# A graph-attention layer: a one-hot pass in front, and the full attention in a dynamic loop behind a test that every block fails

## The chip, the cores and the metric

One core of one Trainium2 chip. The metric is the device time of one execution in microseconds (us), median of several. The profiles come from one execution each; a span is 2 to 4 us shorter than the time of its own run. Engines: TensorE (PE, with its weight loads as PEld), VectorE (DVE), ScalarE (ACT), GpSimd (POOL), SyncE (SP, which here computes nothing and issues most of the DMAs).

## The reference, cut to what matters

```python
def reference(x, adj, W, a):                 # x 4096x512, adj 4096x4096, W 512x(4*512), all float32
    ht  = (x @ W).reshape(N, 4, 512).transpose(1, 0, 2)
    src = einsum('hnd,hd->hn', ht, a[:, :512, 0]);  dst = einsum('hnd,hd->hn', ht, a[:, 512:, 0])
    e   = leaky_relu(src[:, :, None] + dst[:, None, :], 0.01) + adj[None]
    return layernorm(x + mean_over_heads(softmax(e) @ ht))
```

About one entry of adj in 256 is not zero, and those run up to 1e9, while the scores are of the order of tens. So in most rows the largest entry of adj decides the softmax alone. A row's *lead* is how far its largest entry of adj stands above the second.

## The kernel before

It applies the attention rows to x, which stays on chip, and then W. A unit of work is a block of 128 rows with one head. Its scores are made, 512 columns at a time, while the unit before it is in the matrix products:

```python
def add(self, c):        # scores of chunk c, and their largest in each row
    nc.scalar.activation(s, dst_b[:, h, ts(c, C)], AF.Identity, bias=src[:, ib, h : h + 1])
    nc.vector.scalar_tensor_tensor(s, s, SLOPE, s, op0=OP.mult, op1=OP.max)
    nc.vector.tensor_tensor_reduce(out=s, in0=s, in1=adj_t[ib, k][:, ts(part, C)], ...)
    if h == H - 1 and part == AW - 1 and ib + 1 < NB:
        load_adj(ib + 1, k)                  # adj of the next block, as soon as this tile is read
...
for n in range(len(units) + 1):              # 128 units in ONE stream
    after = Unit(n + 1) if n + 1 < len(units) else None
    for c in range(NCH):
        u.transpose(c)                       # 4 transposes, copied by VectorE or ScalarE
        ...                                  # c == 0: before.apply(7), before.scale(); 1: turn; 2: project; 3: store
        u.apply(c - 1)                       # 4 products with x
        after.add(c + 1)                     # scores of the next unit
        ...                                  # its maxima and exponentials at c == 6 and 7
    before, u = u, after
```

Of the kernel before, what the change touches and what calls it, by code (L numbers as in the profile page):

```python
# [9 lines left out]
F32 = mybir.dt.float32  # L10
AF = mybir.ActivationFunctionType
OP = mybir.AluOpType
# [4 lines left out]
LOWEST = -3.4028234663852886e38  # L17


@with_exitstack  # L20
def gat_resnorm_kernel(
# [8 lines left out]
    """layernorm(x + mean_h softmax(leaky_relu(src_i + dst_j) + adj) @ (x @ W_h)).  # L30

    The attention rows are applied to x first and the result to W_h after it:
    x stays on chip for the whole launch, x @ W would not fit. Likewise
    src = x @ (W_h a_src) and dst = x @ (W_h a_dst).
    A unit of work is a block of 128 rows of one head. Its scores are made in
    chunks of 512 columns while the unit before it is in the matrix products.
    """
    nc = tc.nc
    P = 128
    N, D = x.shape  # L40
    H = a.shape[0]
    KB = D // P          # blocks of features
    NB = N // P          # blocks of rows
    C = 512              # columns of a chunk
    NCH = N // C
    Q = C // P           # blocks of rows in a chunk
    AW = 2               # chunks in a tile of adj

    ctx.enter_context(tc.manual_schedule())

    const = ctx.enter_context(tc.tile_pool(name="const", bufs=1))
    x_sb = const.tile([P, NB, D], F32, name="x_sb")
    w_sb = const.tile([P, KB, H * D], F32, name="w_sb")
    dst_b = const.tile([P, H, N], F32, name="dst_b")
    src = const.tile([P, NB, H], F32, name="src")
    ident = const.tile([P, P], F32, name="ident")

    x_blocks = x.rearrange("(nb p) d -> p nb d", p=P)
    w_blocks = W.rearrange("(kb p) m -> p kb m", p=P)

# [1 line left out]
    with ExitStack() as pre:  # L62
        once = pre.enter_context(tc.tile_pool(name="once", bufs=1))
        two = pre.enter_context(tc.tile_pool(name="two", bufs=2))
        pps = pre.enter_context(tc.tile_pool(name="pps", bufs=2, space=bass.MemoryType.PSUM))

        a_b = once.tile([P, H, 2 * D], F32, name="a_b")
        nc.scalar.dma_start(
            a_b.rearrange("p h m -> p (h m)"),
            bass.AP(tensor=a.tensor, offset=a.offset, ap=[[0, P], [1, H * 2 * D]]),  # L70
        )
        for kb in range(KB):
            nc.scalar.dma_start(w_sb[:, kb, :], w_blocks[:, kb, :])
        for g in range(NCH):
            nc.sync.dma_start(x_sb[:, ts(g, Q), :], x_blocks[:, ts(g, Q), :])
        make_identity(nc, ident)

        v = once.tile([P, KB, 2 * H], F32, name="v")
        prod = once.tile([P, D], F32, name="prod")
        for kb in range(KB):  # L80
            for s in range(2):
                for h in range(H):
                    nc.vector.scalar_tensor_tensor(  # L83
                        prod, w_sb[:, kb, ts(h, D)], 1.0, a_b[:, h, ts(s, D)],
                        op0=OP.mult, op1=OP.mult,
                        accum_out=v[:, kb, s * H + h : s * H + h + 1],
                    )

        def x_transposed(g):
            xT = two.tile([P, KB, C], F32, name="xT")  # L90
            for q in range(Q):
                ps = pps.tile([P, KB, P], F32, name="ps_x")
                for kb in range(KB):
                    nc.tensor.transpose(ps[:, kb, :], x_sb[:, g * Q + q, ts(kb, P)], ident)  # L94
                nc.scalar.copy(xT[:, :, ts(q, P)], ps)  # L95
            return xT

        def scores(g, xT):
# [15 lines left out]
        xT = x_transposed(0)  # L114
        for g in range(NCH):
            ahead = x_transposed(g + 1) if g + 1 < NCH else None
            scores(g, xT)
            xT = ahead

# [1 line left out]
    adj_pool = ctx.enter_context(tc.tile_pool(name="adj_pool", bufs=1))  # L121
# [5 lines left out]
    psum = ctx.enter_context(tc.tile_pool(name="psum", bufs=2, space=bass.MemoryType.PSUM))  # L127

    units = [(ib, h) for ib in range(NB) for h in range(H)]
    adj_t, o_ps, norm = {}, {}, {}  # L130

    def load_adj(ib, k):
        t = adj_pool.tile([P, AW * C], F32, name=f"adj{k}")
        nc.sync.dma_start(t, adj[ts(ib, P), ts(k, AW * C)])
        adj_t[ib, k] = t

    class Unit:
        def __init__(self, n):
            self.ib, self.h = units[n]
            self.s = []  # L140
            self.m = stat.tile([P, NCH], F32, name="m")
            self.z = stat.tile([P, NCH], F32, name="z")
            self.nm = stat.tile([P, 1], F32, name="nm")
            self.rz = stat.tile([P, 1], F32, name="rz")
            self.pt = {}
            self.y_ps = None

        def add(self, c):
            """leaky_relu(src + dst) + adj, and its largest in each row."""
            ib, h = self.ib, self.h  # L150
            s = s_pool.tile([P, C], F32, name="s")
            self.s.append(s)
            nc.scalar.activation(s, dst_b[:, h, ts(c, C)], AF.Identity, bias=src[:, ib, h : h + 1])  # L153
            nc.vector.scalar_tensor_tensor(s, s, SLOPE, s, op0=OP.mult, op1=OP.max)  # L154
            k, part = divmod(c, AW)
            nc.vector.tensor_tensor_reduce(  # L156
                out=s, in0=s, in1=adj_t[ib, k][:, ts(part, C)], scale=1.0, scalar=LOWEST,
                op0=OP.add, op1=OP.max, accum_out=self.m[:, c : c + 1],
            )
            if h == H - 1 and part == AW - 1 and ib + 1 < NB:  # L160
                load_adj(ib + 1, k)

        def largest(self):
            nc.vector.tensor_reduce(self.nm, self.m, axis=AX.X, op=OP.max, negate=True)  # L164

        def exp(self, c):
            s = self.s[c]
            nc.scalar.activation(s, s, AF.Exp, bias=self.nm, accum_out=self.z[:, c : c + 1])  # L168

        def transpose(self, c):  # L170
            ps = psum.tile([P, Q, P], F32, name="pt_ps", bufs=3)
            for q in range(Q):
                nc.tensor.transpose(ps[:, q, :], self.s[c][:, ts(q, P)], ident)  # L173
            pt = pt_pool.tile([P, Q, P], F32, name="pt")
            if c in (1, 3, 5):
                nc.scalar.copy(pt, ps)  # L176
            else:
                nc.vector.tensor_copy(pt, ps)  # L178
            self.pt[c] = pt

        def apply(self, c):
            if c == 0:
                self.y_ps = psum.tile([P, D], F32, name="y_ps")
            pt = self.pt.pop(c)
            for q in range(Q):
                nc.tensor.matmul(  # L186
                    self.y_ps, pt[:, q, :], x_sb[:, c * Q + q, :],
                    start=(c == 0 and q == 0), stop=(c == NCH - 1 and q == Q - 1),
                )

        def scale(self):
            """The softmax's divisor, with that of the mean over heads."""
            nc.vector.tensor_reduce(self.rz, self.z, axis=AX.X, op=OP.add)
            nc.vector.tensor_scalar_mul(self.rz, self.rz, float(H))
            nc.vector.reciprocal(self.rz, self.rz)
            self.y = y_pool.tile([P, D], F32, name="y")
            nc.vector.tensor_scalar_mul(self.y, self.y_ps, self.rz)  # L197

        def turn(self):
            ps = psum.tile([P, KB, P], F32, name="yt_ps", bufs=1)  # L200
            for kb in range(KB):
                nc.tensor.transpose(ps[:, kb, :], self.y[:, ts(kb, P)], ident)  # L202
            self.yt = yt_pool.tile([P, KB, P], F32, name="yt")
            nc.scalar.copy(self.yt, ps)  # L204

        def project(self):
            ib, h = self.ib, self.h
            if h == 0:
                o_ps[ib] = psum.tile([P, D], F32, name="o_ps")
            for kb in range(KB):  # L210
                nc.tensor.matmul(  # L211
                    o_ps[ib], self.yt[:, kb, :], w_sb[:, kb, ts(h, D)],
                    start=(h == 0 and kb == 0), stop=(h == H - 1 and kb == KB - 1),
                )
            if h == H - 1:
                r = y_pool.tile([P, D], F32, name="y")
                nc.vector.tensor_add(r, o_ps.pop(ib), x_sb[:, ib, :])  # L217
                st = stat.tile([P, nc.vector.BN_STATS_DIM], F32, name="st")
                nc.vector.bn_stats(st, r)
                mv = stat.tile([P, nc.vector.BN_AGGR_DIM], F32, name="mv")  # L220
                nc.vector.bn_aggr(mv, st)
# [11 lines left out]

    for k in range(NCH // AW):
        load_adj(0, k)
    u = Unit(0)
    for c in range(NCH):
        u.add(c)
    u.largest()
# [61 lines left out]
```

## Time and profile before

| | before |
|---|---|
| median of 2 runs | 4705.72 us |
| busy: TensorE, VectorE, ScalarE | 98%, 45%, 39% |
| time per unit, per block of 4 units | 35.47 us, 141.9 us |
| start to the first load of adj of the attention part | 132.6 us |
| mean granted clock of TensorE | 0.992 |

In the rows of a group, the last two fields are the busy time with the mean length of one, and the idle time of the engine just before the group with what ended it. A row of a timeline gives start, length, engine, source line, operation and operands, and in brackets how long the engine had sat idle and what released it. The lines that carry the reading stand in the prediction below.

### The profile page before, as it was taken

The numbers are of one execution on the slowest core, as the hardware profiler recorded it, in microseconds if no ns is written. First come the engines' busy times: TensorE is split into PE (matmuls) and PEld (weight loads), VectorE is DVE, ScalarE is ACT, GpSimd is POOL, SyncE is SP. The second block draws the span as 40 slices with busy tenths as digits, with TensorE's granted clock in tenths as the row PEclk, the third lists the DMA queues.
The fourth block names the chain that finished last, engine by engine and source line by source line (L and its number), as shares of the span: only waits on it lengthen the run. The fifth ranks groups of instructions, "written<-read, shape, count | busy, mean of one in ns | idle before, by whom it ended". The sixth has DMA issues, their size and how long they took to land.

```text
span 4702.5 us, 38848 instructions
## 1 busy us (share of the span) xinstructions
PE 4596.1 (98%) x14112; PEld 2251.0 (48%) x14112; DVE 2124.3 (45%) x4656; ACT 1811.9 (39%) x3712; POOL 18.2 (0%) x38
## 2 busy tenths in 40 slices
PE   7899999999999999999999999999999999999999
PEld 3344444444444444444444444444444444444444
DVE  3444444444444444444444444444444444444443
ACT  1334334334334434433433433433433443343342
POOL 0000000000000000000000000000000000000000
PEclk7999999999999999999999999999999999999999
DMA  3000000000000000000000000000000000000000
GB/s 125 27 12 21 18 21 20 12 12 21 18 21 20 7 16 21 18 21 16 7 21 21 18 21 16 7 21 21 18 21 12 12 21 21 18 21 12 12 21 3
DMA packets 26127, 92.66 MB, mean 20 GB/s; under 512 B 2768, under 2 KB 2768, under 8 KB 25296
## 3 DMA queue, kind: packets, MB, share of 16 engines
q1 hardware_dynamic: 22656, 75.51, 4.7%
q0 software_dynamic: 2560, 8.39, 0.5%
q10 hardware_dynamic: 720, 6.29, 0.3%
q8 instruction: 111, 1.82, 0.2%
q14 instruction: 80, 0.66, 0.0%
HBM read 81.79 MB, written 8.39 MB: 19 GB/s over the span
## 4 chain that ended last, share of the span: by engine, by line
issue 75%; PE 23%; DVE 1%; POOL 0%; DMA 0%; ACT 0%; POOLq 0%; ACTq 0%; DVEq 0%
PE y_ps L186 16%; PE o_ps L211 2%; PE pt_ps L173 2%; PE ps_b L107 1%; PE ps_sd L101 1%; PE ps_x L94 0%; DVE y L197 0%; DVE prod L83 0%; PE yt_ps L202 0%; POOL out_dram L232 0%; DMA w_sb<-in_L_gnn_W_dram 0%; DVE s L154 0%; DVE sd L103 0%; DVE s L156 0%; PE ps_s L111 0%
## 5 line engine op out<-in xcount | busy, mean ns | idle before, releaser
L186 PE MATMUL y_ps<-x_sb,pt 128*128 128x512 f32 x8192 | 3685.7, 593 | 0.0
L186 PEld LDWEIGHTS y_ps<-x_sb,pt 128*128 128x128 f32 x8192 | 1487.1, 190 | 1531.3 <-issue 1530.9
L154 DVE SCALAR_TENSOR_TENSOR s<-s 128x512 f32<-128x512 f32 x1024 | 705.6, 689 | 1048.4 <-ACT s L153 1006.2
L153 ACT ACTIVATE s<-dst_b,src 128x512 f32<-128x512 f32 x1024 | 723.0, 718 | 971.2 <-PE pt_ps L173 952.2
L178 DVE COPY pt<-pt_ps 128x512 f32<-128x512 f32 x640 | 442.6, 692 | 997.4 <-PE pt_ps L173 997.4
L168 ACT ACTIVATE s<-s,nm 128x512 f32<-128x512 f32 x1024 | 724.0, 708 | 181.0 <-DVE nm L164 181.0
L173 PEld LDWEIGHTS pt_ps<-ident,s 128*128 128x128 f32 x4096 | 512.5, 141 | 551.7 <-issue 538.7
L176 ACT COPY pt<-pt_ps 128x512 f32<-128x512 f32 x384 | 225.1, 586 | 1346.4 <-PE pt_ps L173 1346.4
L156 DVE CUSTOM_DVE_ANT_0 s<-s,adj 128x512 f32<-128x512 f32 x1024 | 708.6, 692 | 35.1
L173 PE MATMUL pt_ps<-ident,s 128*128 128x128 f32 x4096 | 615.3, 273 | 12.7 <-ACT s L168 12.7
L211 PE MATMUL o_ps<-w_sb,yt 128*128 128x512 f32 x1024 | 460.8, 593 | 0.7 <-ACT yt L204 0.7
L211 PEld LDWEIGHTS o_ps<-w_sb,yt 128*128 128x128 f32 x1024 | 184.6, 190 | 184.6 <-issue 183.6
L197 DVE TENSOR_SCALAR y<-y_ps,rz 128x512 f32<-128x512 f32 x128 | 96.0, 750 | 296.8 <-PE y_ps L186 296.8
L168 ACT ACTIVATION_READ_ACCUMULATOR s<-s,nm 128x1 f32 x1024 | 191.2, 187 | 0.0
L202 PE MATMUL yt_ps<-ident,y 128*128 128x128 f32 x512 | 83.9, 286 | 52.6 <-DVE y L197 52.6
L204 ACT COPY yt<-yt_ps 128x512 f32<-128x512 f32 x128 | 75.0, 586 | 76.0 <-PE yt_ps L202 76.0
L202 PEld LDWEIGHTS yt_ps<-ident,y 128*128 128x128 f32 x512 | 53.6, 140 | 83.5 <-DVE y L197 83.5
L224 ACT ACTIVATE sd<-sd 128x1 f32<-128x1 f32 x32 | 6.5, 203 | 210.8 <-DVE sd L223 210.8
L156 DVE DVE_READ_ACCUMULATOR2_ANT m<- 128x1 f32 x1024 | 83.8, 82 | 0.0
L217 DVE TENSOR_TENSOR y<-o_ps,x_sb 128x512 f32<-128x512 f32 x32 | 22.1, 692 | 90.2 <-PE o_ps L211 90.2
L94 PE MATMUL ps_x<-ident,x_sb 128*128 128x128 f32 x128 | 29.9, 422 | 21.8 <-DMA x_sb<-in_x_dram 16.6
L95 ACT COPY xT<-ps_x 128x512 f32<-128x512 f32 x32 | 18.7, 586 | 76.8 <-PE ps_x L94 76.8
(31 smaller groups left out, 412.8 us busy)
## 6 DMA issues: line engine op xcount, KB each, us to landing
adj<-in_adj_dram SPq DMA_DIRECT2D x128, 512.0 KB, 3.4
x_sb<-in_x_dram SPq DMA_DIRECT2D x8, 1024.0 KB, 17.9
out_dram<-y POOLq DMA_DIRECT2D x32, 256.0 KB, 2.3
w_sb<-in_L_gnn_W_dram ACTq DMA_DIRECT2D x4, 1024.0 KB, 10.7
a_b<-in_L_gnn_a_dram ACTq DMA_DIRECT2D x1, 2048.0 KB, 8.8
```

Source lines behind the costliest of these rows:

```text
L153: nc.scalar.activation(s, dst_b[:, h, ts(c, C)], AF.Identity, bias=src[:, ib, h : h + 1])
L154: nc.vector.scalar_tensor_tensor(s, s, SLOPE, s, op0=OP.mult, op1=OP.max)
L156: nc.vector.tensor_tensor_reduce(out=s, in0=s, in1=adj_t[ib, k][:, ts(part, C)], scale=1.0, scalar=LOWEST, op0=OP.add, op1=OP.max, accum_o ...
L168: nc.scalar.activation(s, s, AF.Exp, bias=self.nm, accum_out=self.z[:, c : c + 1])
L173: nc.tensor.transpose(ps[:, q, :], self.s[c][:, ts(q, P)], ident)
L176: nc.scalar.copy(pt, ps)
L178: nc.vector.tensor_copy(pt, ps)
L186: nc.tensor.matmul(self.y_ps, pt[:, q, :], x_sb[:, c * Q + q, :], start=(c == 0 and q == 0), stop=(c == NCH - 1 and q == Q - 1),)
L197: nc.vector.tensor_scalar_mul(self.y, self.y_ps, self.rz)
L202: nc.tensor.transpose(ps[:, kb, :], self.y[:, ts(kb, P)], ident)
L204: nc.scalar.copy(self.yt, ps)
L211: nc.tensor.matmul(o_ps[ib], self.yt[:, kb, :], w_sb[:, kb, ts(h, D)], start=(h == 0 and kb == 0), stop=(h == H - 1 and kb == KB - 1),)
```

## The change

The new kernel first runs a one-hot pass. For each row it finds the largest entry of adj, gathers that row of x, projects and norms it. It then tests for each row whether the lead is larger than anything the scores could add. Blocks in which a row fails would be computed again by the full attention, inside a dynamic loop. In this version the lead asked for is overwritten with 1e30, so every row of every block fails.

```diff
+    leading_rows(tc, x, adj, W, a, out, ident, w_sb, v, n_bad, any_bad)
+    flag = nc.values_load(any_bad[0:1, 0:1], min_val=0, max_val=N)
+    with tc.If(flag > 0, preferred_fallthrough_block=False):
+        general(tc, x, adj, out, ident, w_sb, v, n_bad)
 ...                                         # leading_rows(), new:
+        nc.vector.tensor_scalar(lead_by, lead_by, 0.0, 1e30, op0=OP.mult, op1=OP.add)
 ...
+    for t in range(NB + LAG + 1):           # LAG = 2
+        if t < NB:
+            find_segment(t); row_norm(t)    # reduce 4096 columns to 64 segments, gather the best segment
+        if 0 <= t - 1 < NB:
+            find_column(t - 1)              # the column in it; gather that row of x
+        if 0 <= t - LAG < NB:
+            project(t - LAG); norm(t - LAG)
+        if t < KB:
+            head_vector(t)
 ...                                         # general(): x reloaded, preamble without its look-ahead
-        for g in range(NCH):
-            ahead = x_transposed(g + 1) if g + 1 < NCH else None
-            scores(g, xT)
 ...                                         # block(ib): the old pipeline, but over the 4 units of one block
-    for n in range(len(units) + 1):
+        for n in range(H + 1):
 ...
+    with tc.For_i(0, NB, 1) as ib:
+        here = nc.values_load(n_bad[0:1, ds(ib, 1)], min_val=0, max_val=P)
+        with tc.If(here > 0):
+            block(ib)
```

## The prediction

The prediction's sum came to 400 + 130 + 5520 + 5 = 6055 us, and two terms of it are guesses with no row of the trace behind them: 10 us in (b), for the way from the one-hot pass into the code behind it, so that the 130 is 10 + 5 + 115; and 6.5 us per block in (c), for the turn of the loop, so that the 172.5 is 166.0 + 6.5. Together they make 10 + 32 x 6.5 = 218 us; without them the sum would be 5837.

> **What bounds the kernel now.** I read the busy table first, then the costliest groups, then the timeline of one unit of work (a block of 128 rows with one head; there are 32 x 4 = 128 of them) in the middle, and last the two ends of the trace.
>
> ```profile
> PE 4596.1 (98%) x14112; PEld 2251.0 (48%) x14112; DVE 2124.3 (45%) x4656; ACT 1811.9 (39%) x3712; POOL 18.2 (0%) x38
> ...
> L186 PE MATMUL y_ps<-x_sb,pt 128*128 128x512 f32 x8192 | 3685.7, 593 | 0.0
> ```
>
> TensorE is busy 98% of the span and its largest group has no idle time before it, while VectorE and ScalarE are under half. So the matrix products bound it. The timeline of TensorE gives the period:
>
> ```profile
> 1035.23 0.60 PE L173 MATMUL pt_ps<-ident,s 128*128 128x128 f32 x4
> 1036.24 0.66 PE L202 MATMUL yt_ps<-ident,y 128*128 128x128 f32 x4 [0.41 <-DVE y L197]
> 1036.73 3.60 PE L186 MATMUL y_ps<-x_sb,pt 128*128 128x512 f32 x8
> ...
> 1070.70 0.60 PE L173 MATMUL pt_ps<-ident,s 128*128 128x128 f32 x4
> ```
>
> The same place of the next unit comes 1070.70 - 1035.23 = 35.47 us later, with 0.41 us of waiting in it. Scores, maxima and exponentials of the next unit lie wholly beside it; that is what the software pipeline over units buys. The filling and draining of that pipeline are seen only once each, and the change makes them happen 32 times, so these are the rows that matter. Filling, at the first unit (first score, first adj sum, first exponential, first transpose, then the first transpose of the second unit):
>
> ```profile
> 137.59 5.01 ACT L153 ACTIVATE s<-dst_b,src 128x512 f32<-128x512 f32 x8 [19.02 <-PE ps_s L111]
> ...
> 139.07 0.69 DVE L156 CUSTOM_DVE_ANT_0 s<-s,adj 128x512 f32<-128x512 f32 x1
> ...
> 149.36 0.72 ACT L168 ACTIVATE s<-s,nm 128x512 f32<-128x512 f32 x1 [6.76 <-DVE nm L164]
> ...
> 150.23 1.97 PE L173 MATMUL pt_ps<-ident,s 128*128 128x128 f32 x8 [12.73 <-ACT s L168]
> ...
> 179.92 0.60 PE L173 MATMUL pt_ps<-ident,s 128*128 128x128 f32 x4
> ```
>
> From the first sum with adj to the first transpose are 150.23 - 139.07 = 11.16 us, all VectorE's 8 chunks of two passes each; TensorE idles 12.73 us. Draining, at the last unit:
>
> ```profile
> 4681.96 7.03 PE L186 MATMUL y_ps<-x_sb,pt 128*128 128x512 f32 x16
> 4689.84 0.66 PE L202 MATMUL yt_ps<-ident,y 128*128 128x128 f32 x4 [0.84 <-DVE y L197]
> 4691.22 3.70 PE L211 MATMUL o_ps<-w_sb,yt 128*128 128x512 f32 x8 [0.73 <-ACT yt L204]
> ...
> 4697.26 0.55 DVE L231 TENSOR_SCALAR y<-y,mv,sd 128x512 f32<-128x512 f32 x1
> ```
>
> The last product ends at 4681.96 + 7.03 = 4688.99, the normed row block is ready at 4697.81: 8.82 us in which one engine at a time works.
>
> [...]granted clock 0.50 in the stretch 140 to 145 us, where TensorE idles, and 1.00 from 176 us. The eight products after that gap took 4.72 us against 3.60 later.[...] The 512 KB adj loads here take 3.4 us in the median[...], and the loads at the start move 385 to 440 GB/s[...].
>
> **The change part by part.** The added test subtracts 1e30 from every row's lead, so no row passes: all 32 blocks go to the attention code, and the one-hot results are overwritten. Nothing is saved; everything new is added. The order of instructions of the changed program confirms that a block holds the same 288 products and transposes as four units of before, inside a loop with one body, one condition[...].
>
> (a) *The one-hot pass*, in front and almost alone. Traffic: adj 67.1 MB, x 8.4, gathered x 8.4, output 8.4, W and a 6.3, gathered segments 1.1, in all 99.7 MB; at 400 GB/s (the start of the trace) 250 us. VectorE per block: a reduction over 4096 columns, about 4.4 us (estimate: 692 ns for 512 columns less 0.16 fixed, times 8, plus 0.16), nine small operations at 0.15 to 0.2, statistics 0.69, some waits: 7.6 us, 243 us in all, plus 32 x 0.73 = 23 us for the head vectors. So either bounds it near 270. But the order is strict: the gather of x for block t-2 starts after the column is found in step t-1, and VectorE takes the norm of that block in step t right after its next column. One step is thus at least gather plus projection: gather about 5 us (2.3 us for a store of 256 KB here, more under load and behind the other gather), transposes 0.6, copy and waits 1.1, four fp32 products at 0.86 warm or 1.72 cold. That is 10 to 14 us; 32 x 12 = 384, with start and end I take **400 us**, by far the least certain term (290 to 480).
>
> (b) *Branch, reload and preamble.* [...] x is loaded again, its first 1 MB in about 5 us, the rest hidden. A group of the old preamble took 13.5 us (transposes at 60.07, 73.58, 87.10). The change drops the transposing one group ahead, which puts the last copy (0.59 us and two hops) on the path: 14.4 us, times 8 = 115. Sum **130 us**, where before spent 137 on loads and preamble together.
>
> (c) *A block of the loop.* Loads of adj can no longer run ahead. First tile after 3.5 us, then 11.16: 14.7 us until the first transpose. TensorE: 29.69 for the first unit (179.92 - 150.23, cold clock included), two units at 35.47, and from the last unit's first transpose (4649.92) to the last product's end 39.07: 139.7. Drain 8.8. Store 0.5 to issue and 2.3 to land[...]: 2.8. Sum from rows of the trace 166.0. [...] **172.5 us**, times 32 = **5520 us**. Before, a block cost 4 x 35.47 = 141.9, so a block loses 30.6 us, 980 in all. The table loads for exponential and square root (1.28 us) stay hidden behind the sums and the projection.
>
> Sum: 400 + 130 + 5520 + 5 for the end = **6055 us**, 1.29 times before.
>
> **The rivals.** *The loop overlaps its blocks*: if the engines were held only by their own data, the next block's loads and scores would run under the last product, and a block would stay near 142 to 150 us, in all about 5200. Against it: [...]adj has one buffer per tile. *The one-hot pass runs at its bandwidth*: 270 instead of 400, in all 5925. For it: adj has six buffers, so the loads run far ahead; against it the two-step chain above. [...] *The branch isn't taken*, and only the one-hot pass runs, under 500 us: the numbers written into the test rule it out (a finite bound times 0 plus 1e30).
>
> **Range and chances.** The block is uncertain by 4 us either way (128 us in all), the one-hot pass by about 90, the preamble by 10; together about 155 as independent errors, a little skewed upward by the loop's turn. Range **5920 to 6240 us** for 8 in 10. Even the most favourable rival is 10% slower than before, so slower by over 2% has a chance of 0.98, within 2% 0.01, faster 0.01 (only if the branch doesn't fire).
>
> **What would show each step right or wrong.** Thirty-two equal periods: the first transposes of the blocks some 172 us apart, TensorE idle some 30 us between a block's last product and the next block's first transpose, granted clock 0.5 at the head of each block and 1.00 in it. TensorE's busy share near 78 to 80%, its work in the loop almost that of before. In the first 400 us: DMA well under full share and VectorE waiting for TensorE before the statistics if my chain is right; full share and under 300 us if the bandwidth rival is. A group of the preamble near 14.4 us. It would be wrong if adj of the next block arrives before the current one ends, if the gap between blocks is far from 33 us, or if the one-hot pass is over 500 us, for which the gathers would have to be several times slower than the stores of before.

In (a), 0.86 us is (7.03 - 3.60) / 4, from the products of the draining rows, and 1.72 an estimate, its double: in the same trace the weight loads of the preamble's products stand 0.85 us apart at the granted clock 0.50 (78.15 and 79.00 us) and 0.43 apart at 1.00 (79.93 and 80.36).

## The result

| | before | changed |
|---|---|---|
| median of 2 runs | 4705.72 us | 5947.19 us (5943.91 and 5950.47) |
| ratio of fast runs | 1 | 1.2636, 95% interval 1.2612 to 1.2660 |
| span of the profiled run | 4702.5 us | 5941.6 us |
| mean granted clock | 0.992 | 0.918 |

A ratio is the mean time of one kernel's fast runs over that of the other's fast runs of the same rounds, so it is not quite the ratio of the medians. The changed kernel is slower, and within the predicted range, in its lower part (27 us above the lower end, 108 below the middle).

From the page of the changed kernel, the busy line and two groups, then the second group as the page of the kernel before has it:

```profile
PE 4902.0 (83%) x14567; PEld 2384.1 (40%) x14568; DVE 2339.5 (39%) x5122; ACT 1881.3 (32%) x3877; POOL 77.4 (1%) x87
...
L380 PE MATMUL y_ps<-x_sb,pt 128*128 128x512 f32 x8192 | 3722.0, 598 | 0.2
...
L367 PE MATMUL pt_ps<-ident,s 128*128 128x128 f32 x4096 | 639.1, 282 | 732.1 <-ACT s L362 732.1
```

```profile
L173 PE MATMUL pt_ps<-ident,s 128*128 128x128 f32 x4096 | 615.3, 273 | 12.7 <-ACT s L168 12.7
```

The products are as many as before and nearly as long. What is new is in the row of L367: the transposes have 732.1 us of idle time before them, released by an exponential, where before they had 12.7. 732.1 / 32 = 22.9 us per block. The timeline of all engines at the turn from one block to the next:

```profile
697.01 0.55 DVE L421 TENSOR_SCALAR y_g<-y_g,mv_g,sd_g 128x512 f32<-128x512 f32 x1
697.59 0.37 SPq L422 DMA_DIRECT2D out_dram<-y_g  x1
...
702.45 2.25 SPq L328 DMA_DIRECT2D adj<-in_adj_dram  x4
...
706.76 0.69 DVE L352 CUSTOM_DVE_ANT_0 s<-s,adj 128x512 f32<-128x512 f32 x1 [3.02 <-DMA adj<-in_adj_dram]
...
717.93 1.97 PE L367 MATMUL pt_ps<-ident,s 128*128 128x128 f32 x8 [23.24 <-ACT s L362]
```

The normed rows are ready at 697.56 us. The first load of adj is issued at 702.45, 4.89 us later; VectorE waits 3.02 us for it; and 15.48 us after that issue TensorE starts. The first transposes of the first and of the last block stand at 548.27 and 5788.21 us, so a block takes (5788.21 - 548.27) / 31 = 169.03 us, against 141.9 before: 27.1 us lost per block.

The spans split like this: the last product of the one-hot pass ends at 409.05 us and the loop's first load is issued at 532.76, so

| part | before | changed | predicted for changed |
|---|---|---|---|
| one-hot pass | - | 409.1 | 400 |
| join, reload, preamble | 132.6 | 123.7 | 130 |
| attention of 32 blocks, with the end | 4569.9 | 5408.8 | 5525 |

For the one-hot pass, the timeline at one step (the gather of a block's rows of x, the transposes that wait for it, the statistics that wait for the projection):

```profile
342.73 0.95 POOL L156 DMA_INDIRECT y<-in_x_dram,col  x1 [0.31 <-issue]
...
351.78 1.09 PE L166 MATMUL tp<-ident,y 128*128 128x128 f32 x4 [6.26 <-DMA y<-in_x_dram,col]
...
358.71 0.70 DVE L178 BATCH_NORM_STATS2 st<-o 128x6 f32<-128x512 f32 x1 [5.74 <-PE o L172]
```

The column is found just before the gather's issue; the statistics of the gathered rows can begin 16 us later, in the next step, and VectorE waits 5.74 us for the projection before them.

### The profile page after: what moved, and what is told of

It reads as the page before. It is cut to its first block, busy times and chain, and to the rows that moved or that the text cites. A ratio compares the mean times of both kernels' runs of the same rounds, so it can differ in the third digit from the quotient of the medians.

```text
span 5941.6 us, 44197 instructions
## 1 busy us (share of the span) xinstructions
PE 4902.0 (83%) x14567; PEld 2384.1 (40%) x14568; DVE 2339.5 (39%) x5122; ACT 1881.3 (32%) x3877; POOL 77.4 (1%) x87
## 5 line engine op out<-in xcount | busy, mean ns | idle before, releaser
L367 PE MATMUL pt_ps<-ident,s 128*128 128x128 f32 x4096 | 639.1, 282 | 732.1 <-ACT s L362 732.1
L367 PEld LDWEIGHTS pt_ps<-ident,s 128*128 128x128 f32 x4096 | 530.9, 146 | 1264.0 <-ACT s L362 757.9
L347 ACT ACTIVATE s<-dst_b,src_i 128x512 f32<-128x512 f32 x1024 | 701.7, 716 | 886.3 <-PE pt_ps L367 708.2
L362 ACT ACTIVATE s<-s,nmx 128x512 f32<-128x512 f32 x1024 | 724.0, 708 | 430.2 <-DVE nmx L358 430.2
L405 PE MATMUL o_ps<-w_sb,yt_g 128*128 128x512 f32 x1024 | 463.9, 596 | 23.4 <-ACT yt_g L398 23.4
L405 PEld LDWEIGHTS o_ps<-w_sb,yt_g 128*128 128x128 f32 x1024 | 184.4, 190 | 214.6 <-issue 183.7
L391 DVE TENSOR_SCALAR y_g<-y_ps,rz 128x512 f32<-128x512 f32 x128 | 96.1, 751 | 403.2 <-PE y_ps L380 403.2
L398 ACT COPY yt_g<-yt_ps 128x512 f32<-128x512 f32 x128 | 75.0, 586 | 542.8 <-PE yt_ps L396 542.8
L362 ACT ACTIVATION_READ_ACCUMULATOR s<-s,nmx 128x1 f32 x1024 | 191.3, 187 | 0.0
L172 PE MATMUL o<-w_sum,yt 128*128 128x512 f32 x256 | 146.3, 724 | 14.2 <-ACT yt L168 14.2
L133 DVE TENSOR_REDUCE seg<-adj_t 128x64 f32<-128x4096 f32 x32 | 141.2, 4412 | 10.9 <-DMA adj_t<-in_adj_dram 10.9
L396 PE MATMUL yt_ps<-ident,y_g 128*128 128x128 f32 x512 | 84.0, 287 | 66.2 <-DVE y_g L391 66.2
```

Source lines behind the costliest of these rows:

```text
L133: nc.vector.tensor_reduce(seg, adj_t.pop(ib).rearrange("p (s e) -> p s e", e=E), axis=AX.X, op=OP.max)
L172: nc.tensor.matmul(o, yt[:, kb, :], w_sum[:, kb, :], start=False, stop=(kb == KB - 1))
L347: nc.scalar.activation(s, dst_b[:, self.h, ts(c, C)], AF.Identity, bias=src_i[:, self.h : self.h + 1])
L362: nc.scalar.activation(s, s, AF.Exp, bias=self.nm, accum_out=self.z[:, c : c + 1])
L367: nc.tensor.transpose(ps[:, q, :], self.s[c][:, ts(q, P)], ident)
L396: nc.tensor.transpose(ps[:, kb, :], self.y[:, ts(kb, P)], ident)
```

## The experiments

All twelve kernels gave a correct result. The kernel before took 4704 to 4708 us.

### 1. Does the one-hot pass cost what the trace says? (a1)

```diff
-        nc.vector.tensor_scalar(lead_by, lead_by, 0.0, 1e30, op0=OP.mult, op1=OP.add)
```

> The line that sets the asked lead to 1e30 is taken out, nothing else. On these inputs the bound on what the scores can add is about 65 and the smallest lead of a row is 10880, so no row should fail and neither the reload nor the loop should run. Theory (the three parts of the changed kernel lie one after another and don't disturb each other): the one-hot pass alone, ended at about 412 us in the changed kernel's trace, so 412 to 422 us, with a correct result. Rival (the pass is slowed or helped by what stands behind it, or some block fails): over 700 us with one failing block, or a pass that differs from 410 by more than 10 us.

Measured: 414.60 us (414.07 without the one slow run), ratio to before 0.0881 (0.0879 to 0.0883), span 410.2. The pass alone takes what it takes in front of the loop (409.1). So the parts lie one after another and their costs add up. It also shows what the test is for: with the true bound no row of these inputs fails, and the kernel is 11 times faster than the one before.

### 2. What bounds a step of the one-hot pass? (b1, b2, b3)

b1, on a1:

```diff
         if 0 <= t - LAG < NB:
             project(t - LAG)
-            norm(t - LAG)
+        if 0 <= t - LAG - 1 < NB:
+            norm(t - LAG - 1)
```

> The kernel a1 with the norm of a block one step later (step t takes the norm of block t-3 in place of t-2); the projection stays at t-2. Theory (a step is as long as the chain column, gather, projection, because VectorE waits for the projection in the next step): the chain now has two steps, so a step falls from about 12 us to VectorE's own work, some 7.6 us, or the transfers' 7.3 us, and the pass to 270 to 300 us. Rival (the pass is held by bandwidth, that is by gathers that queue behind the large loads): the step stays near 12 us and the time above 380 us.

Measured: 351.86 us (350.74 without the one slow run), ratio 0.0742 (0.0739 to 0.0746), between the two forecasts (whose 7.3 us for the transfers is an estimate: a step's 2.92 MB at the prediction's 400 GB/s). The mean distance between the large reductions, from the fifth to the last, fell from 10.75 us in a1 to 8.82. The wait for the projection fell from 107.6 us (30 times) to 8.7 (2 times), but a new one stands in its place. From b1's groups:

```profile
L183 DVE RECIPROCAL sd<-sd 128x1 f32<-128x1 f32 x32 | 5.2, 164 | 53.6 <-ACT sd L182 53.6
...
L178 DVE BATCH_NORM_STATS2 st<-o 128x6 f32<-128x512 f32 x32 | 22.1, 692 | 8.7 <-PE o L172 8.7
```

ScalarE's square root stands in its queue behind the copy of the transposed rows of a younger block, and that copy waits for the gather. So b2 moves the norm ahead of the projection in the order of a step:

```diff
+        if 0 <= t - LAG - 1 < NB:
+            norm(t - LAG - 1)
         if 0 <= t - LAG < NB:
             project(t - LAG)
-        if 0 <= t - LAG - 1 < NB:
-            norm(t - LAG - 1)
```

> The kernel b1, with the norm of block t-3 ahead of the projection of block t-2 in the order of a step. In b1's trace VectorE no longer waits for the products, but 53.6 us for ScalarE's square root, which stands behind the copy of the transposed gathered rows, and that copy waits for the gather. Theory (what is left of the chain in b1 is ScalarE's order alone): that wait goes, a step falls to VectorE's 7.4 us or the transfers' 7.3 us, the time to 285 to 310 us. Rival (the gathers, which take 3 to 8 us to land behind the loads of adj, hold the step by way of the buffers of x): the time stays over 330 us.

Measured: 335.49 us, ratio 0.0714 (0.0711 to 0.0716). The wait for the square root fell from 53.6 to 12.9 us, and the mean step to 7.73 us; the wait for the projection came back in part, from 8.7 to 24.9 us (10 times). Three reductions in b2's timeline of VectorE, one 7.32 us after another:

```profile
226.57 4.41 DVE L133 TENSOR_REDUCE seg<-adj_t 128x64 f32<-128x4096 f32 x1
...
233.90 4.41 DVE L133 TENSOR_REDUCE seg<-adj_t 128x64 f32<-128x4096 f32 x1
...
241.22 4.41 DVE L133 TENSOR_REDUCE seg<-adj_t 128x64 f32<-128x4096 f32 x1
```

So most steps are as the theory had them, and the total is not; taken alone it falls under the rival (over 330 us). I had left out the four slow first steps (78 us until the fifth reduction) and the end after the last reduction (46 us). One wait at the start looked like plain waste, 18.4 us of VectorE until the vectors of a land. b3 forms the head vectors in steps 8 to 11:

```diff
-        if t < KB:
-            head_vector(t)
+        if 8 <= t < 8 + KB:
+            head_vector(t - 8)
```

> The kernel b2 with the head vectors formed in steps 8 to 11 in place of steps 0 to 3. In b2's trace a step in the middle takes 7.3 us, as its theory said, but VectorE waits 18.4 us at the start for the vectors of a, whose load lands late behind the first loads of adj; the expectation for b2 had left start and end out. Theory (that wait is lost time): it goes, the time falls by 15 to 20 us to about 317 us. Rival (the first loads bound the start in any case, and the work of 23 us comes back later): within 5 us of 335.

Measured: 337.89 us, ratio 0.0718 (0.0715 to 0.0721): no gain. The fifth reduction began at 56.08 us in place of 77.94, but the four steps that now carry the head vectors took 13 us each, and the last reduction began at 291.68 in place of 286.77. The rival was right that the wait bought nothing. What sets the 335 us is then not settled; between the start and the end of b2, in its stretch 100 to 300 us, VectorE is busy 85% and the DMA engines 88%.

### 3. The turn of the loop (c1, d1)

c1 uses the true test and makes block 0 alone fail, so 31 turns skip the body:

```diff
         nc.vector.tensor_scalar(gap, gap, 0.0, None, op0=OP.is_gt)
+        nc.vector.memset(gap[:, 0:1], 0.0)
```

> The true test, but block 0 is set to fail in all its rows: the join, the reload, the preamble and one full block run, and the loop turns 31 times more with its body skipped. Theory (a turn[...] costs about 2.7 us, the rest of the 4.9 us from a store's issue to the next load's is the store itself): 533 + 169 + 31 x 2.7 = 786 us. Rival (the turn is nearly all of the 4.9 us): 533 + 169 + 152 = 854 us.[...]

Measured: 821.74 us, between the theory and its rival. The theory's 2.7 us was an estimate, 4.9 less some 2.2 for the store; the stores of the kernel before took 2.3 us to land. In its trace block 0's store is issued at 702.97 us and the span ends at 819.5: 116.5 us for 31 empty turns and the end, at most 3.76 us per turn. The larger instruction queue moved 0.15 MB in all, as in the changed kernel, where all 32 turns run the body.

d1 takes the changed kernel and replaces loop and inner condition by 32 copies of the block:

```diff
-    with tc.For_i(0, NB, 1) as ib:
-        here = nc.values_load(n_bad[0:1, ds(ib, 1)], min_val=0, max_val=P)
-        with tc.If(here > 0):
-            block(ib)
+    for ib in range(NB):
+        block(ib)
```

> The changed kernel with the dynamic loop and the inner condition replaced by 32 copies of the same block, in the same order of instructions. Theory (what a block loses is mostly that VectorE and ScalarE end one block before they begin the scores of the next in program order; the loop's turn of 4.9 us and the wait for adj of 3 us are the smaller part): a block falls from 169 to about 160 us, the whole to about 5655 us. Rival (the barrier of the loop is what keeps blocks apart; without it the engines overlap them): a block near 142 to 146 us, the whole 5080 to 5200 us.

Measured: 5820.20 us, 127 less than the changed kernel but 165 more than the theory, and 165.36 us per block. So the turn costs 169.03 - 165.36 = 3.7 us, in agreement with c1, and the loop is not what keeps the blocks apart: the rival falls. But I had expected the wait for adj to go too, and it stayed. d1's timeline:

```profile
688.38 0.35 SPq L422 DMA_DIRECT2D out_dram<-y_g  x1
...
688.84 1.81 SPq L328 DMA_DIRECT2D adj<-in_adj_dram  x4
...
693.47 0.69 DVE L352 CUSTOM_DVE_ANT_0 s<-s,adj 128x512 f32<-128x512 f32 x1 [3.55 <-DMA adj<-in_adj_dram]
```

The loads of the next block are issued 0.46 us after the store of this one: both stand in SyncE's queue, which goes in order, and the store waits for the last rows of the block.

### 4. Loads ahead (d2)

```diff
-            nc.sync.dma_start(out[ds(ib * P, P), :], r)
+            nc.gpsimd.dma_start(out[ds(ib * P, P), :], r)
```

> The unrolled kernel d1 with the store of a block issued by GpSimd in place of the queue that loads adj. In d1 the loads of the next block stood behind the store in that queue's order and began only 0.46 us after it, so VectorE still waited 3.55 us for the first tile; the expectation for d1 had missed that. Theory: the loads now run ahead, this wait goes, and nothing else: 165.4 - 3.6 = 161.8 us per block, in all 5818 - 32 x 3.6 = 5703 us. Rival (with the queue free the blocks overlap as in the kernel before): near 5100 us. Rival (the tiles of adj come free too late to matter): no change from 5820 us.

Measured: 5712.14 us. The turn from block to block in d2; the first sum with adj no longer waits:

```profile
691.78 0.55 DVE L421 TENSOR_SCALAR y_g<-y_g,mv_g,sd_g 128x512 f32<-128x512 f32 x1
692.24 0.16 DVE L331 COPY src_i<-src 128x4 f32<-128x4 f32 x1
692.44 5.01 ACT L347 ACTIVATE s<-dst_b,src_i 128x512 f32<-128x512 f32 x8 [0.89 <-DVE src_i L331]
...
693.19 0.69 DVE L350 SCALAR_TENSOR_TENSOR s<-s 128x512 f32<-128x512 f32 x1 [0.79 <-ACT s L347]
693.92 0.69 DVE L352 CUSTOM_DVE_ANT_0 s<-s,adj 128x512 f32<-128x512 f32 x1
```

A block takes 161.6 us (mean of the 31 distances, 161.13 to 162.23), 3.8 less than in d1. Still no overlap between blocks: 19.7 us more than before remain, with neither loop nor wait for adj. The rows show the link: ScalarE's first score of the next block waits for src_i (the source scores of that block's rows), which VectorE copies, in its own order, right after the norm of the block before.

### 5. One stream, and fewer turns (e1, f1, f2)

All three share one edit, shown by its core, which makes the units of G blocks one stream and loads adj of the next block during the last head.

```diff
-    def block(ib):
+    def group(first, G):
+        units = [(j, h) for j in range(G) for h in range(H)]
 ...
+                if self.h == H - 1 and part == AW - 1 and self.j + 1 < G:
+                    load(self.j + 1, k)
 ...
-        for n in range(H + 1):
+        for n in range(len(units) + 1):
```

The edit also doubles two buffers, src_i and o_ps (the sum of the projections). That was not run alone, but src_i is copied without a wait in d2's rows above, and o_ps is first written a unit after a block's start. e1 calls `group(0, NB)` with no loop. f1 and f2 keep the loop with steps of 2 and 4 and test only the first block's count, which is right only because all blocks fail here.

> The changed kernel with loop and inner condition replaced by the units of all 32 blocks in one stream, as in the kernel before (the next unit's scores beside this unit's products, adj of the next block loaded during the last head). Theory (the loop's cost is that filling and draining are exposed once a block): 533 us to the loop's start, 15.5 + 29.6 + 126 x 35.47 + 39.1 + 12 = 4565 us, so about 5100 us, 845 us less than the changed kernel. Rival (the code after the one-hot pass is slower in itself, by its buffers or its place): 5250 us or more.

> The dynamic loop kept, with two blocks streamed in one turn (16 turns, condition on the first block's count only; right here, where all fail). Theory: a turn costs one exposed filling and draining, 169.0 us for its first block and 4 x 35.47 = 141.9 for the second, so 533 + 16 x 310.9 = 5510 us. Rival (the loss belongs to each block, not to each turn): near 5940 us.

> As f1 with four blocks in a turn (8 turns). Theory of a fixed loss of 27.1 us per turn: 533 + 8 x (169.0 + 3 x 141.9) = 5291 us. Rival[...], with the instruction queue's bytes many times the 0.15 MB of the changed kernel.

| blocks per turn | turns | expected | measured | from turn to turn |
|---|---|---|---|---|
| 1 (the changed kernel) | 32 | - | 5947.19 | 169.0 |
| 2 (f1) | 16 | 5510 | 5498.36 | 310.6 |
| 4 (f2) | 8 | 5291 | 5301.16 | 596.1 |
| 32, no loop (e1) | - | 5100 | 5106.48 | - |

The loss goes with the turns, not with the blocks: 310.6 is 169.0 + 141.9 within 0.3, and e1 takes 841 us off. The idle time before the transposes, 732.1 us with 32 turns, is 362.8 with 16 and 186.6 with 8; in e1 it is left once:

```profile
L376 PE MATMUL pt_ps<-ident,s 128*128 128x128 f32 x4096 | 615.2, 273 | 15.5 <-ACT s L371 15.5
```

In f2 the instruction queues move more. The larger one in the changed kernel and in f2 (packets, MB, share):

```profile
q8 instruction: 9, 0.15, 0.0%
```

```profile
q8 instruction: 126, 2.06, 0.2%
```

In f1 it moved 0.21 MB; without a loop it moved 1.82 MB (the kernel before) and 1.88 MB (d1). The second instruction queue, q14, rose in f2 as well, from 0.08 to 0.80 MB. Yet f2's turn is only 596.1 - (169.0 + 3 x 141.9) = 1.4 us longer than the sum, and it was not shown that even these come from the queues. (Of f2's rival, the queue's bytes rose as it had them.)

### 6. The cold clock at the head of a block (h1, h2)

h1 keeps TensorE busy while it would idle:

```diff
+        warm = psum.tile([P, KB, P], F32, name="yt_ps", bufs=1)
+        for _ in range(14):
+            nc.tensor.matmul(warm.rearrange("p k c -> p (k c)"), ident, x_sb[:, 0, :], start=True, stop=True)
         u = Unit(0)
```

> The changed kernel with 14 products whose results nobody reads (128x512 in float32, the identity with a block of x) issued at the head of each block, where TensorE idles. Theory (the cold clock at the head of a block costs the first 29.6 us about 1.5 us): the first eight products and transposes run at full clock, each block is 1.2 to 1.7 us shorter, in all 5890 to 5908 us against 5947. Rival (the clock falls back before the first transposes, or is not what stretches the first unit): within 10 us of 5947.

Measured: 5939.25 us, ratio to before 1.2620 (1.2599 to 1.2641), which overlaps the changed kernel's interval: no gain that can be told, as the rival had it. The clock did warm up: granted 0.50 in the stretch 715 to 718 us of the changed kernel, 1.00 in h1. The theory's 1.5 us was an estimate; the rows of this turn give (1.97 - 1.36) + (4.27 - 3.70) = 1.18 us. TensorE's timeline of h1 shows where it went:

```profile
718.04 1.36 PE L367 MATMUL pt_ps<-ident,s 128*128 128x128 f32 x8 [0.62 <-ACT s L362]
719.48 3.70 PE L380 MATMUL y_ps<-x_sb,pt 128*128 128x512 f32 x8
723.02 0.60 PE L367 MATMUL pt_ps<-ident,s 128*128 128x128 f32 x4
724.67 3.70 PE L380 MATMUL y_ps<-x_sb,pt 128*128 128x512 f32 x8 [1.05 <-ACT pt L370]
```

The first products take 3.70 in place of 4.27 us, and then TensorE waits 1.05 us for a copy that ScalarE has behind eight exponentials and two scores. h2 issues the exponentials of the first unit only two chunks ahead:

```diff
-        for c in range(NCH):
+        for c in range(2):
             u.exp(c)
 ...
                     u.transpose(c)
+                if n == 0 and c + 2 < NCH:
+                    u.exp(c + 2)
```

> The kernel h1, with the exponentials of a block's first unit issued two chunks ahead of their transposes in place of all eight at once. In h1's trace the clock is 1.00 at the first transposes and the first products are 0.57 us shorter, yet the second group of products starts no earlier, as the copy of chunk 1 on ScalarE stands behind the eight exponentials and two scores (TensorE waits 1.05 us for it). Theory (the gain of the clock was turned into this wait): it goes, 1.0 to 1.3 us per block, the whole 5895 to 5910 us. Rival (the first unit is held by something else as well): over 5925 us.

Measured: 5888.75 us, ratio 1.2518 (1.2497 to 1.2539), clear of h1 and a little better than the theory. h2's timeline, first block:

```profile
548.38 1.05 PE L367 MATMUL pt_ps<-ident,s 128*128 128x128 f32 x8
...
553.74 3.60 PE L380 MATMUL y_ps<-x_sb,pt 128*128 128x512 f32 x8
```

From the first transposes to the second group of products are now 553.74 - 548.38 = 5.36 us (6.63 in h1's block above). Over all 32 blocks the mean is 7.12 us in the changed kernel, 6.77 in h1 and 5.46 in h2. The clock was 1.00 at the first transposes of every block of h1 and h2, but it fell back to 0.50 within 8 us of them in 13 blocks of h1 and in one of h2, the second, which took 7.04 us (its first products took 5.33 us in place of 3.70; 5.29 in h1's block at 5611.87). In the 19 blocks of h1 where it stayed up the stretch still took 6.63, so the order on ScalarE, not the fall of the clock, held h1 there. From turn to turn h1 takes 168.76 us, h2 167.32, the changed kernel 169.03. The gain came with the exponentials' order and the warm clock together; the order alone, with a cold clock, was not run.

## Why the prediction was right

**The bound and the whole-block loss: right.** The units inside a block run as before (the three last units' rows repeat before's to 0.01 us). A block loses 27.1 us, where the prediction said 30.6. The experiments split it by removing one thing at a time:

| piece of the 27.1 us | size | from |
|---|---|---|
| turn of the loop | 3.7 | d1 against the changed kernel; c1 agrees |
| adj can't be loaded ahead | 3.8 | d2 against d1 |
| pipeline filled and drained once per block | 19.7 | d2 (161.6) against a block of before (141.9); e1 gives it back |

About 1.7 us of the block is recovered by h2's warm clock and order. That overlaps the last piece and isn't added to it.

**Filling and draining: right to within 0.8 us.** From the first transpose to the last product 140.0 us in the mean (139.55 to 140.88; predicted 139.7), drain 8.81 (8.8), first load to first transpose 15.5 (14.7; the first tile could be used 4.3 us after its issue, not 3.5).

**The turn: the term that was mis-sized.** The 2.8 us of the store (0.5 to issue and 2.3 to land) plus the 6.5, in all 9.3, measured 4.8 in the mean from the normed rows to the next load (4.89 in the turn shown). Three things in it were wrong. The store is issued 0.03 us after the normed rows, not 0.5. SyncE waits only 21.7 us in 32 turns, 0.68 each, for the landing of the store, so most of that lies beside its other work of the turn. And the 6.5 us were a guess: a turn costs 3.7 (d1), and the larger instruction queue moved the same 0.15 MB with 32 full turns as with 31 empty ones (c1). 4.5 us less here, 0.8 more for the first tile and 0.3 more for the products leave 3.5 per block (172.5 - 169.03), 111 us in 32, and that is the distance between 6055 and the measured 5947 (108): the other errors, 9 us too little for the one-hot pass and 6 too much for the preamble, nearly cancel. The gap from the last product to the next first transposes, which the prediction named as 33 us, came out at 29.1.

**The one-hot pass: the sum right, its pieces not.** 400 was predicted and 409.1 measured. The chain through the gather was the right cause: VectorE waits 113.8 us in 30 steps for the projection, and b1 and b2, which take the chain apart, bring the mean step from 10.75 to 8.82 and 7.73 us. But a step in the middle takes 11.0 us in the changed kernel, not 12, and the fifth begins only at 80 us; the two errors cancelled, so that the sum fits this well is luck. The largest piece of the chain is the gather, 3.3 to 9.6 us from issue to landing (median 6.0), where I had taken 5.

**Reload and preamble: right**, 123.7 for 130; from the last product of the one-hot pass to the first transposes of the reloaded x were 7.55 us, 6.2 of them after the first load's issue, for a predicted 10 + 5, and a group took 447.56 - 432.87 = 14.69 us, the next three 14.35, 14.73 and 14.25, for a predicted 14.4.

**Rivals.** That blocks overlap once only data hold them was wrong even without a loop (d1, d2), since ScalarE and VectorE take a block's last rows before the next block's first scores in their own order. So the reason that the prediction gives against it, the one buffer per tile of adj, is not what decides, and neither is the loop: d1 has no loop, d2's loads run ahead with the same buffers, and neither overlaps. That the one-hot pass runs at its bandwidth was wrong: 409.1 us, with the DMA engines busy 64% of the first 405 us. TensorE's share came out at 83%, above the 78 to 80 I named, as I hadn't counted its 215 us in the one-hot pass.

The experiments also point to a version that beats both: b2, the one-hot pass with the true test and the later norm, at 335.49 us. Its fallback is kept, but only c1, which has the order of a1 and not of b2, ran the fallback with the true bound, and its failing block was forced.

## What to carry to other kernels

A software pipeline is worth what its fill and drain cost times how often they occur (here 27.1 us in each of 32 turns, 3.7 of them the turn itself): before putting a pipelined body into a dynamic loop, read the first and the last unit in the trace of the unlooped kernel and multiply, and give a turn of the loop several trips of work. Unrolling (d1) and freeing the loads (d2) did not bring overlap back, because the order of instructions on each engine ends one trip before the next begins. A wait removed on one engine (the projection in b1, the cold clock in h1) came back both times as the queue order of another engine, so look at what releases the next instruction before calling the first theory wrong.
